# The last stage of a two-layer graph model: weights and two blocks of rows loaded during attention, projections one block further ahead

## The chip, the core and the metric

The kernel runs on one core of a Trainium2 chip. The metric is device time in microseconds (us); less is better. The engines are named as in the profile: PE is the matrix engine (PEld its weight loads, which overlap), DVE the vector engine, ACT the scalar engine, POOL the GpSimd engine, and SP the engine that issues nearly all DMAs here. Each engine runs its own instructions in order, and engines wait for one another by semaphores. SBUF is the on-chip memory, PSUM the small memory into which PE writes[...].

## The reference

A graph attention network of two layers is followed by one masked transformer layer. The change lies in the transformer layer, which is computed from x, the output of the graph layers (4096 rows of 256):

```
qkv = layer_norm(x, g1, be1) @ w_qkv              # 8 heads of 32
scores = einsum('nhd,mhd->hnm', q, k) * SCALE
scores = where(adj != 0, scores, -inf)
attn = softmax(scores, axis=-1)
out = einsum('hnm,mhd->nhd', attn, v).reshape(n, 256)
x = x + out @ w_proj + b_proj
h2 = layer_norm(x, g2, be2)
ff = gelu(h2 @ w1 + b1) @ w2 + b2                 # 256 -> 1024 -> 256
return x + ff
```

## The kernel before

The first half of the time goes to the graph layers, which the change does not touch. The transformer layer is the function `unshifted_transformer`. It works on the 4096 rows in eight blocks of 512 (`NNB`, `NB`), and on the eight heads in two halves of four (`DC`, `HC`). There are three parts.

**Queries, keys and values.** For each block, PE multiplies the normed rows by the weights (L1668, L1687). Queries and keys are split into a high and a low fp16 half and written to DRAM (`half_d`). From there `stack` reads the keys back into one large tile, `k_st`, of 128 partitions by 8 heads by 4096 columns: two DMAs of 32 partitions for each block (L1624), each followed by a copy on DVE to the 32 partitions beside it (L1701). Values stay in `v_sb`. In this part the order of SP's instructions is the written one.

**Attention.** The work is cut into 512 units: block of queries `nb`, half of the heads `c`, and one of 32 tiles of 128 keys `mt`. For each unit and each pair of heads (`u`), `weights` does eight matmuls into PSUM (L1725), an exponential on ACT (L1732) and a product with the mask on DVE (L1734), which gives a tile `u_e` (a ring of ten). POOL adds the tiles of two units that follow each other into `u_both` (L1816, a ring of six), except for two pairs of every sixteen. PE then multiplies `u_e` by the values (`u_av`) and `u_both` by ones (`u_dn`), both at L1743; a list, `waiting`, interleaves these with later units' scores. At the end of each half of the heads ACT copies both sums out; the numerators go to `att_d` in DRAM (L1760), the denominators to `den_d` (L1778). Two later steps read the denominators back in another shape (L1781) and invert them on DVE and store them in `inv_d` (L1785, L1786). The order on PE, ACT and DVE is the written one; on SP and POOL it is set by the scheduler of the language, which works with its own estimates of durations. All 512 units have the same length, so one half of the heads of one block takes about 73 us. Query tiles (`u_q`) and masks (`u_mask`) have rings of two and five buffers; the masks are read in four chunks per block.

**The last stage.** After attention, the projection weights, the biases and the feed-forward weights are loaded (L1840 to L1898; the projection weights twice). For each block `rows_of` issues six DMAs: the rows of x (L743, `u_xres`), the attention numerators (L1861, `u_att`) and four with the inverted denominators, spread over the partitions (L1866, `u_wide`). `projected` adds the projection bias on POOL (L1874), multiplies numerators and inverses on DVE (L1875), does 16 projection matmuls (L1879), adds the result to the rows (L1886) and norms them: the mean on DVE (L1447, L1448), squares on ACT (L1455), a square root on ACT (L1462), reciprocal and scaling on DVE (L1473, L1475). POOL then adds the second bias (L1889). `turned` transposes the normed rows on PE (L1488), evicted by ACT (L1491). In the profile a matmul of fp32 counts as two, so 16 written ones appear as 32.

The loop over blocks is written like this: the projection of block `nb + 1`, whose rows are also loaded there; 16 matmuls into the hidden layer (L1915) with a gelu on ACT (L1922); the transposes of block `nb + 1`; 32 matmuls out of the hidden layer (L1931) with an add on DVE (L1938) and stores on SP (L1939). Before the loop block 0 is projected and transposed. The order in this stage is the scheduler's on all engines, and what it chose on PE is, for each block: hidden layer, transposes of the next block, output layer, projection of the block after the next one.

```
        res, res_n = projected(*first)
        hn = turned(res_n)
        for nb in range(NNB):
            more = nb + 1 < NNB
            if more:
                res_next, res_n = projected(*rows_of(nb + 1))
```

Tiles of a pool with two buffers (`u_xres`, `u_att`, `u_wide`) can be loaded only when the block two before has let go of them; for `u_xres` this is when its output has been stored.

Of the kernel before, what the change touches and what calls it, by code (L numbers as in the profile page):

```python
# [8 lines left out]
F32 = mybir.dt.float32  # L9
BF = mybir.dt.bfloat16  # L10
F16 = mybir.dt.float16
# [1547 lines left out]
def unshifted_transformer(  # L1559
# [46 lines left out]
    nc.vector.memset(ones, 1.0)  # L1606
    dens = wts.tile([P, NQ, QI], F32, name="u_dens")


    with ExitStack() as scope:  # L1610
        vals = scope.enter_context(tc.tile_pool(name="u_vals", bufs=1))
        k_st = vals.tile([P, DC * HC, N], F16, name="u_k")
        v_sb = vals.tile([P, NT, D], F32, name="u_v")
        blocks = scope.enter_context(tc.tile_pool(name="u_blocks", bufs=2))
        masks = scope.enter_context(tc.tile_pool(name="u_masks", bufs=5))
        block_tiles = {}

        def stack(to, i, order, cols):

            for a, kind in enumerate(order):  # L1620
                if kind is None:
                    continue
                first = half_d[i, kind, 0, 0:1, cols]
                nc.sync.dma_start(  # L1624
                    to[a * O : (a + 1) * O],
                    spread(first, [[N, O], [O * N, DC * HC], [1, NB]]),
                )

        def load_queries(nb):
            q_st = blocks.tile([P, DC * HC, NB], F16, name="u_q")  # L1630
            stack(q_st, 0, (0, 1, 0, 1), slice(nb * NB, (nb + 1) * NB))
            block_tiles[nb] = q_st, []
# [9 lines left out]
        with ExitStack() as qkv:  # L1642
# [8 lines left out]
            for nb in range(NNB):  # L1651
# [44 lines left out]
                for b in (nb - 1,) if nb + 1 < NNB else (nb - 1, nb):  # L1696
                    if b >= 0:
                        at = slice(b * NB, (b + 1) * NB)
                        stack(k_st[:, :, at], 1, (0, None, 1, None), at)
                        for o in (0, 2 * O):  # L1700
                            nc.vector.tensor_copy(k_st[o + O : o + 2 * O, :, at], k_st[o : o + O, :, at])  # L1701
                    if b == 0:
                        load_queries(0)
# [12 lines left out]
        def weights(nb, c, mt, u):  # L1716

            q_st, chunks = block_tiles[nb]
            mask = chunks[mt // MC][:, mt % MC, :].unsqueeze(1).to_broadcast([P, 2, NB])
            ps = ps_s.tile([P, 2, NB], F32, name="u_ps")  # L1720
            for j in range(2):
                h = c * HC + 2 * u + j
                for r in range(HC):
                    at = mt * P + r * O
                    nc.tensor.matmul(  # L1725
                        ps[r * O : (r + 1) * O, j, :],
                        k_st[:, h, at : at + O],
                        q_st[:, h, :],
                        start=True,
                        stop=True,  # L1730
                    )
            nc.scalar.activation(ps, ps, AF.Exp, scale=SCALE)  # L1732
            e = work.tile([P, 2, NB], F32, name="u_e")
            nc.vector.scalar_tensor_tensor(e, mask, 0.0, ps, op0=ALU.not_equal, op1=ALU.mult)  # L1734
            return e
# [55 lines left out]


        units = [(nb, c, mt) for nb in range(NNB) for c in range(DC) for mt in range(NT)]
        es_of = {}
# [10 lines left out]
        for i in range(len(units) + 5):  # L1805
            for u in range(HC // 2):
                if i < len(units):
                    nb, c, mt = units[i]
                    if u == 0 and c == DC - 1 and mt % MC == 2 and nb + 1 < NNB:
                        if mt < MC:  # L1810
                            load_queries(nb + 1)
                        load_chunk(nb + 1, mt // MC)
                    es_of.setdefault(i, []).append(weights(*units[i], u))
                    if i % 2 == 1 and not alone(mt):
# [10 lines left out]
                for _ in range(min(count, len(waiting))):  # L1825
                    waiting.pop(0)()
            if i % 2 == 0 and later:
                later.pop(0)()
# [5 lines left out]
    with ExitStack() as scope:  # L1834
# [3 lines left out]
        ps_m = scope.enter_context(tc.tile_pool(name="u_ps_m", bufs=8, space=PSUM))  # L1838
        wp_sb = big.tile([P, DC, D], F32, name="u_wp")
        nc.sync.dma_start(wp_sb, w_proj.rearrange("(c p) e -> p c e", p=P))  # L1840

        def by_row(src, name):
            t = big.tile([P, D], F32, name=name)
            nc.sync.dma_start(t, spread(src, [[0, P], [1, D]]))
            return t.unsqueeze(1).to_broadcast([P, TB, D])

        bp_sb = by_row(b_proj, "u_bp")
        wp_sb = big.tile([P, DC, D], F32, name="u_wp")
        nc.sync.dma_start(wp_sb, w_proj.rearrange("(c p) e -> p c e", p=P))


        inside = big.tile(list(dens.shape), F32, name="u_inside")
        nc.vector.tensor_scalar(inside, dens, DEN_MIN, DEN_MAX, op0=ALU.max, op1=ALU.min)
        nc.vector.tensor_tensor(inside, inside, dens, op=ALU.is_equal)
        nc.vector.tensor_reduce(checks.column(), inside, AX.XY, ALU.min)

        def rows_of(nb):
            res = tail.tile([P, TB, D], F32, name="u_xres")
            rows.load(res, nb * TB)
            att = tail.tile([P, DC, NB], F32, name="u_att")  # L1860
            nc.sync.dma_start(  # L1861
                att, att_d[:, :, nb * NB : (nb + 1) * NB].rearrange("c p n -> p c n")
            )
            inv = tail.tile([P, DC, NB], F32, name="u_wide")
            for j in range(HC):
                nc.sync.dma_start(  # L1866
                    inv[j * O : (j + 1) * O],
                    spread(inv_d[nb * DC, j : j + 1, :], [[0, O], [HC * NB, DC], [1, NB]]),
                )
            return res, att, inv  # L1870

        def projected(res, att, inv):

            nc.gpsimd.tensor_tensor(res, res, bp_sb, op=ALU.add)  # L1874
            nc.vector.tensor_tensor(att, att, inv, op=ALU.mult)  # L1875
            for t in range(TB):
                pp = ps_m.tile([P, NB], F32, name="misc")
# [13 lines left out]


        first = rows_of(0)
        b2_sb = by_row(b2, "u_b2")
        w1_sb = big.tile([P, DC, F], F32, name="u_w1")
        nc.sync.dma_start(w1_sb, w1.rearrange("(c p) f -> p c f", p=P))
        w2_sb = big.tile([P, FC, D], F32, name="u_w2")
        nc.sync.dma_start(w2_sb, w2.rearrange("(c p) e -> p c e", p=P))  # L1898
        def turned(res_n):
# [4 lines left out]

        res, res_n = projected(*first)
        hn = turned(res_n)
        for nb in range(NNB):
            more = nb + 1 < NNB
            if more:
                res_next, res_n = projected(*rows_of(nb + 1))  # L1910
            hid = tail.tile([P, FC, NB], F32, name="u_hid")
# [13 lines left out]
            if more:  # L1925
                hn = turned(res_n)
            for t in range(TB):
# [13 lines left out]
                )  # L1941
            if more:
                res = res_next

# [109 lines left out]
```

## Time and profile before

| | us |
|---|---|
| median of 3 runs | 3249.26 (3246.59 to 3256.77) |
| profiled execution, its own time | 3250.22 |
| span of the profiled execution, first to last instruction | 3248.4 |
| PE busy | 3099.1 (95%) |
| DVE busy | 2804.6 (86%) |
| ACT busy | 2703.1 (83%) |
| POOL busy | 1177.5 (36%) |
| end of attention on PE, from the start of the span | 2946.4 |
| last matmul of the last stage ends | 3240.75 |

The times come from one execution that the hardware profiler recorded; they are counted from the start of its span. A row of the chain of work names a piece of work that ended just before the next one could start, so the pieces add up to the time. A row of the timeline gives the start, the length and the number of instructions that follow each other closely, and in brackets how long the engine stood idle before and who ended that. "SPq" is the issue of a DMA on SP, not its transfer. "Clock" is the share of PE's full clock that was granted.

### The profile page before, as it was taken

The page shows a single profiled execution, that of the slowest core. Times are in us where ns is not written, and L with a number is a line of the kernel's source. Part 1 is how long each engine was busy: PE and PEld are TensorE (multiplying, and loading weights), DVE is VectorE, ACT ScalarE, POOL GpSimd, SP SyncE. Part 2 cuts the span into 40 slices and gives each one's busy share as a digit, 9 for nine tenths or more (in the row PEclk, how much of TensorE's full clock was granted, in tenths as well). Part 3 has the DMA queues.
Part 4 walks back from the last instruction along what each step waited for, and adds up shares of the span by engine and source line. Part 5 has one row for each costly group of instructions (what it writes and reads, how often), then busy time and mean ns, then how long its engine had stood idle before and what let it go on. Part 6 is the DMA issues. An engine that isn't in the chain of part 4 may idle for free.

```text
span 3248.4 us, 139142 instructions
## 1 busy us (share of the span) xinstructions
PE 3099.1 (95%) x64076; PEld 2717.4 (84%) x64076; DVE 2804.6 (86%) x3102; ACT 2703.1 (83%) x3305; POOL 1177.5 (36%) x536
## 2 busy tenths in 40 slices
PE   5899999999889999999988999999999999997999
PEld 4799999999779999999965888888888888885666
DVE  6899999988889999999966999999999999994121
ACT  5799999999679999999964888888888888884332
POOL 2300000000310000000002998999888998893110
PEclk8999999999999999999999999999999999998999
DMA  7666554420310213120145010101101010004200
GB/s 250 203 198 201 167 185 149 148 74 29 105 42 31 84 54 93 42 75 27 38 121 143 14 40 20 33 27 27 32 24 47 14 40 15 20 7 120 69 33 27
DMA packets 210306, 249.30 MB, mean 77 GB/s; under 512 B 87792, under 2 KB 131056, under 8 KB 209712
## 3 DMA queue, kind: packets, MB, share of 16 engines
q1 hardware_dynamic: 209712, 240.31, 24.1%
q8 instruction: 503, 8.24, 1.1%
q14 instruction: 91, 0.75, 0.1%
HBM read 197.80 MB, written 42.47 MB: 74 GB/s over the span
## 4 chain that ended last, share of the span: by engine, by line
PE 44%; ACT 4%; DVE 3%; DMA 2%; issue 1%; POOL 0%; SPq 0%; POOLq 0%; DVEq 0%; ACTq 0%
PE u_ps L1725 15%; PE u_av L1743 14%; PE u_dn L1743 8%; PE misc L1931 3%; ACT t L1100 2%; PE misc L1668 2%; PE misc L1915 1%; PE misc L1687 1%; DMA u_xres<-rows 1%; DVE t L1102 1%; DVE t L1115 1%; PE misc L1488 1%; ACT ln_square L1455 0%; POOL u_xres L1874 0%; PE misc L1879 0%
## 5 line engine op out<-in xcount | busy, mean ns | idle before, releaser
L1401 PE MATMUL bank<-vst,t 128*128 128x132 f16 x16384 | 1451.0, 220 | 32.0 <-DVE t L1115 31.5
L1816 POOL TENSOR_TENSOR u_both<-u_e 128x1024 f32<-128x1024 f32 x448 | 1052.5, 2391 | 934.0 <-DVE u_e L1734 931.7
L1401 PE MATMUL bank<-vst,mask 128*128 128x66 f16 (+1 forms) x10296 | 1345.3, 206 | 0.0
L1100 ACT ACTIVATE t<-s_b,g_terms 128x1024 int8<-128x1024 f32 x1231 | 1318.9, 1154 | 27.6 <-PE bank L1401 21.7
L1401 PEld LDWEIGHTS <-t 128*128 128x128 fp8e4 x16384 | 1183.5, 97 | 47.1 <-DVE t L1115 36.6
L1734 DVE SCALAR_TENSOR_TENSOR u_e<-u_mask,u_ps 128x1024 f32<-128x1024 uint8 x1024 | 1165.9, 1215 | 10.3 <-ACT u_ps L1732 6.9
L1732 ACT ACTIVATE u_ps<-u_ps 128x1024 f32<-128x1024 f32 x1024 | 1030.1, 1009 | 142.1 <-PE u_ps L1725 44.0
L1401 PEld LDWEIGHTS <-mask 128*128 128x128 fp8e4 x10296 | 903.5, 98 | 0.0
L1115 DVE SCALAR_TENSOR_TENSOR t<-mask,t 128x2048 int32<-128x2048 int32 x256 | 591.3, 2310 | 82.6 <-ACT t L1100 72.4
L1725 PE MATMUL u_ps<-u_q,u_k 128*32 128x512 f16 x8192 | 637.1, 383 | 11.9 <-DVE u_e L1734 11.2
L1743 PE MATMUL u_av<-u_e,u_v 128*32 128x128 f32 x16384 | 601.8, 273 | 0.6 <-issue 0.6
L1743 PEld LDWEIGHTS u_av<-u_e,u_v 128*32 128x32 f32 x16384 | 488.9, 110 | 129.5 <-issue 2.6
L1102 DVE TENSOR_SCALAR t<-s_b,g_terms 128x1024 fp8e4<-128x1024 f32 x817 | 583.8, 747 | 2.6 <-DMA s_b<-s_d 2.6
L1035 POOL TENSOR_TENSOR vst<-g_prod,vst 128x528 f16<-128x528 f32 x36 | 44.2, 1244 | 777.8 <-DVE vst L1034 757.4
L1743 PE MATMUL u_dn<-u_both,u_ones 128*32 128x128 f32 x7168 | 280.2, 273 | 0.0
L1725 PEld LDWEIGHTS <-u_k 128*32 128x32 f16 x8192 | 228.6, 95 | 57.4 <-issue 16.2
L1743 PEld LDWEIGHTS u_dn<-u_both,u_ones 128*32 128x32 f32 x7168 | 212.9, 110 | 41.1 <-issue 0.5
L1922 ACT ACTIVATE u_hid<-misc,n_b 128x512 f32<-128x512 f32 x64 | 42.7, 682 | 149.5 <-PE misc L1915 149.5
L1938 DVE TENSOR_TENSOR u_xres<-u_xres,misc 128x256 f32<-128x256 f32 x32 | 13.5, 421 | 121.1 <-PE misc L1931 121.1
L1931 PE MATMUL misc<-u_w,u_hid 128*128 128x256 f32 x512 | 111.8, 379 | 0.0
L1915 PE MATMUL misc<-ln_cols,u_w 128*128 128x512 f32 x256 | 111.2, 592 | 0.0
L1931 PEld LDWEIGHTS misc<-u_w,u_hid 128*128 128x128 f32 x512 | 96.8, 190 | 13.2 <-issue 0.5
(147 smaller groups left out, 1916.4 us busy)
## 6 DMA issues: line engine op xcount, KB each, us to landing
g_adj<-in_adj_dram SPq DMA_DIRECT2D x123, 512.0 KB
s_b<-s_d SPq DMA_DIRECT2D x64, 512.0 KB
mask<-mask SPq DMA_DIRECT2D x128, 256.0 KB
u_mask<-mask SPq DMA_DIRECT2D x32, 512.0 KB
mask<-stage SPq DMA_DIRECT2D x48, 256.0 KB
rows<-e_x SPq DMA_DIRECT2D x32, 256.0 KB
half_d<-u_halves SPq DMA_DIRECT2D x32, 256.0 KB
u_q<-half_d SPq DMA_DIRECT2D x32, 256.0 KB
```

The source lines that it names most:

```text
L1100: nc.scalar.activation(to.bitcast(I8), s, AF.Sign, bias=negd, scale=-1.0)
L1102: nc.vector.tensor_scalar(to, s, negd, -1.0, op0=ALU.is_ge, op1=ALU.mult, saturate=False)
L1115: nc.vector.scalar_tensor_tensor(both, m32.unsqueeze(1).to_broadcast(list(both.shape)), SIGNS, both, op0=ALU.bitwise_or, op1=ALU.bitwise_and,)
L1401: nc.tensor.matmul(to, left, right, start=k not in opened, stop=last)
L1668: nc.tensor.matmul(pq, wq_sb[k][:, i * D + c * P : i * D + (c + 1) * P], hn[:, k, :], start=(k == 0), stop=(k == DC - 1),)
L1725: nc.tensor.matmul(ps[r * O : (r + 1) * O, j, :], k_st[:, h, at : at + O], q_st[:, h, :], start=True, stop=True,)
L1732: nc.scalar.activation(ps, ps, AF.Exp, scale=SCALE)
L1734: nc.vector.scalar_tensor_tensor(e, mask, 0.0, ps, op0=ALU.not_equal, op1=ALU.mult)
L1743: nc.tensor.matmul(to[j * O : (j + 1) * O, at], lefts[j], es[j // 2][:, j % 2, at], start=first and part == 0, stop=last and part == PARTS ...
L1816: nc.gpsimd.tensor_tensor(both, es_of[i - 1][u], es_of[i][u], op=ALU.add)
L1915: nc.tensor.matmul(ph, w1_sb[:, k, f * P : (f + 1) * P], hn[:, k, :], start=(k == 0), stop=(k == DC - 1),)
L1931: nc.tensor.matmul(po[:, :D], hid[:, f, at : at + P], w2_sb[:, f, :], start=(f == 0), stop=(f == FC - 1),)
```

## The change

The pools `u_blocks` (query tiles) and `u_masks` are kept open until the end, and the keys become two tiles, one for each half of the heads. The first lies in a pool of its own, `u_slab`. So each block's keys are stacked with four DMAs and four DVE copies of half the size, instead of two and two.

The second tile of `u_slab` takes the place of the first half's keys once these are no longer read, which is when the first half of the heads of the last block has its scores. `load_early` cuts it up and loads into it the projection weights, two biases, block 0's rows, numerators and inverses, and the feed-forward weights. Block 1's are loaded into a query buffer and a mask buffer that the last block doesn't use. POOL adds the projection bias to the rows of both blocks and multiplies numerators and inverses during attention; the duplicate load of the projection weights goes. ACT takes one square root of a single column ahead of its last two copies of attention.

In the last stage PE's order is now the written one. Blocks 0 and 1 are projected at once, block 0 is transposed, and then the loop projects block `nb + 2` ahead of the hidden layer of block `nb`, and loads block `nb + 3`. `u_xres` has four buffers. The checks of the denominators (`inside`) are written behind the first transposes.

In the scheduled program the instructions that the scheduler places stand so. On SP block 1's six loads stand behind the last block's mask loads, and before the stores of block 6's last sums. The loads of the slab up to block 0's inverses stand behind the next inverses' store; w1 stands behind the numerators' store of the last block's first half, and w2 between the four denominator stores (L1794) and the denominator load (L1797) of that half. On POOL the product for block 1 stands behind the first two sums (L1868) of the last block's first half; the two bias adds (L1882) stand ahead of the first two sums of its second half, and the product for block 0 (L1885) behind these two.

```diff
+    rooted = wts.tile([P, 1], F32, name="u_rooted")
+    slab_p = ctx.enter_context(tc.tile_pool(name="u_slab", bufs=1))
+    blocks = ctx.enter_context(tc.tile_pool(name="u_blocks", bufs=2))
+    masks = ctx.enter_context(tc.tile_pool(name="u_masks", bufs=5))
+    def load_rows(nb, res, att, inv):
+        rows.load(res, nb * TB)
+        nc.sync.dma_start(att, att_d[:, :, nb * NB : (nb + 1) * NB].rearrange("c p n -> p c n"))
+        for j in range(HC):
+            nc.sync.dma_start(
+                inv[j * O : (j + 1) * O],
+                spread(inv_d[nb * DC, j : j + 1, :], [[0, O], [HC * NB, DC], [1, NB]]),
+            )
...
-        k_st = vals.tile([P, DC * HC, N], F16, name="u_k")
+        k_st = [
+            pool.tile([P, HC, N], F16, name=f"u_k{c}") for c, pool in enumerate((slab_p, vals))
+        ]
...
-                        stack(k_st[:, :, at], 1, (0, None, 1, None), at)
-                        for o in (0, 2 * O):
-                            nc.vector.tensor_copy(k_st[o + O : o + 2 * O, :, at], k_st[o : o + O, :, at])
+                        for c in range(DC):
+                            stack(k_st[c][:, :, at], 1, (0, None, 1, None), at, c, HC)
+                            for o in (0, 2 * O):
+                                nc.vector.tensor_copy(
+                                    k_st[c][o + O : o + 2 * O, :, at], k_st[c][o : o + O, :, at]
+                                )
...
+        def load_early():
+            slab = slab_p.tile([P, 32 * D], F32, name="u_k0")
...
+            early["wp"] = piece(DC, "p (c e) -> p c e", c=DC)
+            nc.sync.dma_start(early["wp"], w_proj.rearrange("(c p) e -> p c e", p=P))
+            for name, src in (("bp", b_proj), ("b2", b2)):
+                early[name] = piece(1, "p (o e) -> p o e", o=1)
+                nc.sync.dma_start(early[name][:, 0], spread(src, [[0, P], [1, D]]))
+            two = blocks.tile([P, 2, TB * D], F32, name="u_q")
+            early[0] = (
+                piece(TB, "p (t d) -> p t d", t=TB),
+                piece(TB, "p (c n) -> p c n", c=DC),
+                piece(TB, "p (c n) -> p c n", c=DC),
+            )
+            early[1] = (
+                two[:, 0].rearrange("p (t d) -> p t d", t=TB),
+                two[:, 1].rearrange("p (c n) -> p c n", c=DC),
+                masks.tile([P, DC, NB], F32, name="u_mask"),
+            )
+            for nb in range(2):
+                load_rows(nb, *early[nb])
+            early["w1"] = piece(FC, "p (c f) -> p c f", c=DC)
+            nc.sync.dma_start(early["w1"], w1.rearrange("(c p) f -> p c f", p=P))
+            early["w2"] = piece(FC, "p (f e) -> p f e", f=FC)
+            nc.sync.dma_start(early["w2"], w2.rearrange("(c p) e -> p c e", p=P))
...
+                    if u == 0 and units[i] == (NNB - 1, DC - 1, 4):
+                        load_early()
...
+            for k, unit in enumerate(((NNB - 1, DC - 1, NT // 2 - 1), units[-1])):
+                if i < len(units) and units[i] == unit:
+                    res, att, inv = early[k]
+                    nc.gpsimd.tensor_tensor(
+                        res, res, early["bp"].to_broadcast([P, TB, D]), op=ALU.add
+                    )
+                    nc.gpsimd.tensor_tensor(att, att, inv, op=ALU.mult)
+            if i == len(units) - 1:
+                nc.scalar.activation(rooted, norms.eps, AF.Sqrt)
...
         def rows_of(nb):
-            res = tail.tile([P, TB, D], F32, name="u_xres")
+            res = tail.tile([P, TB, D], F32, name="u_xres", bufs=4)
...
+            load_rows(nb, res, att, inv)
             nc.gpsimd.tensor_tensor(res, res, bp_sb, op=ALU.add)
             nc.vector.tensor_tensor(att, att, inv, op=ALU.mult)
+            return res, att
...
-        res, res_n = projected(*first)
-        hn = turned(res_n)
+        scope.enter_context(tc.manual_schedule(engines={mybir.EngineType.PE}))
+        ready = [projected(*early[nb][:2]) for nb in range(2)]
+        coming = rows_of(2)
+        hn = turned(ready[0][1])
...
         for nb in range(NNB):
+            res, res_n = ready.pop(0)
             more = nb + 1 < NNB
-            if more:
-                res_next, res_n = projected(*rows_of(nb + 1))
+            if nb + 2 < NNB:
+                ready.append(projected(*coming))
+                if nb + 3 < NNB:
+                    coming = rows_of(nb + 3)
...
             if more:
-                hn = turned(res_n)
+                hn = turned(ready[0][1])
```

In the changed kernel the projection matmuls are at L1917, the hidden layer at L1957, the output layer at L1973, its adds at L1980, and the reciprocal of the denominators at L1801.

## The prediction

> **What bounds the kernel now.** I read the page's chain first, then the chain in order of time around the end of attention, then windows and timeline there. On the page the chain that ended last is matmul work almost throughout:
>
> ```profile
> PE 44%; ACT 4%; DVE 3%; DMA 2%; issue 1%; POOL 0%; SPq 0%; POOLq 0%; DVEq 0%; ACTq 0%
> ```
>
> So TensorE decides, and a change pays where TensorE stands still. Two windows (length, then busy us and count of PE, PEld, DVE, ACT, POOL, then clock, DMA share, GB/s) compare attention with what follows it:
>
> ```profile
> 2880.00:2909.00 29.00, 29.00 (x828) 22.78 (x822) 29.00 (x28) 25.81 (x26) 25.74 (x12) 1.00 0.02 5
> 2949.00:2966.00 17.00, 5.46 (x13) 4.37 (x14) 3.74 (x8) 0.00 (x0) 2.34 (x1) 0.51 0.75 245
> 3000.00:3240.00 240.00, 233.01 (x862) 159.15 (x861) 43.39 (x101) 74.97 (x134) 28.19 (x12) 1.00 0.14 44
> ```
>
> Attention has PE and DVE both full and POOL nearly so; the start of the last stage is empty and at half clock; the rest of it is 97% PE. The chain in order of time (start, us, what) across the seam and one later block:
>
> ```profile
> 2944.64 1.78 PE u_dn L1743 x62
> ...
> 2947.96 5.24 DMA den_d<-u_den
> 2953.28 1.75 DMA u_dens<-den_d
> 2956.66 3.88 DMA u_b<-in_L_gnn_b_dram
> 2960.54 6.60 PE misc L1879 x16
> ...
> 2976.16 5.63 PE misc L1879 x16
> 2981.79 13.73 PE misc L1915 x32
> 2995.52 0.88 PE misc L1488 x8
> 2996.39 13.83 PE misc L1931 x64
> ...
> 3012.55 3.96 DMA u_xres<-rows
> 3016.67 2.36 POOL u_xres L1874
> 3028.86 1.63 PE misc L1488 x8
> 3030.49 13.83 PE misc L1931 x64
> ```
>
> Attention ends at 2946.4; the first feed-forward matmul (L1915) starts at 2981.8, 35.4 us later, behind denominators, weights, two projections and a layer norm. Thereafter each block's transposes (L1488) wait for a norm whose rows were loaded only after the previous block's output: 2996.4 to 3030.5 is 34.1 us of pitch.
>
> **The last stage, step by step.** Let 0 be attention's end. With weights and both blocks' inputs in place, the first projection needs only the copy of the denominators out of PSUM (0.59, done at 0.65). At full clock 16 projection matmuls take 3.62 (PE timeline at 3010.05), so projections 0 and 1 end at 4.3 and 7.9. DVE adds (0.42 each) end for block 0 at 4.8; mean 1.23, one add of block 1 in between, scaling 0.18: 6.7. Four squares at 0.63: 9.2. The square root's table load (1.28) has been moved ahead of the last copies, where ACT sat idle 3.7 us in the old trace, so the root takes 0.3: 9.6. Meanwhile DVE finishes block 1's adds and mean at 9.65. Reciprocal, scaling, two norm pieces (0.35 each), the last reciprocal of denominators (its data arrived 8.6 after attention's end in the old trace; it isn't late), two more pieces: 11.7. Transposes end near 12.2.
>
> PE's order then puts the projection of **block 2** ahead of block 0's feed-forward. Its attention product stands on DVE behind four small checks (1.5 in all, to 13.2) and block 1's norm; the latter waits for ACT, which does block 1's squares and block 0's two evictions (0.72 each) first: root at 14.55, norm to 16.2, product 1.22 to 17.45. Its loads were issued from 2.3 on; the last quarter follows the reciprocal and should land near 13, hidden.
>
> PE has by then been almost idle for 5 us or more. After the old seam the granted clock read 0.5 from 2949.3, and with work from 2960.5 it recovered at 2966.4, 5.9 us later. By that row block 2's projection runs at half clock, 5.6 to 6.6 as in the two rows above; I take 6.1, and feed-forward starts at **23.6**. [...] Thus 35.4 - 23.6 = **11.8** saved.
>
> The third projection is then already done, where the old kernel had done two: one of 3.28 (3010.22 to 3013.50) fewer remains: **3.3**.
>
> From L1915's start to PE's last L1931 (3240.75) the old stage took 258.96. Its pieces are 8 x 13.73 + 8 x 13.83 + 7 x 0.88 + 6 x 3.28 = 246.3, so 12.6 were waits for rows and norms. Afterwards projection runs two blocks ahead, the norm of block nb+1 has some 30 us, and ACT's 12.6 us per block (8 x 0.68, 4 x 0.69, two table loads, root, two evictions) fits the 32 us pitch. The new order has one snag, a gelu table load waiting for the first hidden tile, 1.28 late[...]. I take all **12.6**; if only the first half of the waits goes it is 6. The tail of 7.65 us stays. Sum: 11.8 + 3.3 + 12.6 = **27.7**.
>
> **What is put into attention.** The early loads are 17 DMAs on SP (6 for block 1's rows, attention and inverses; 3 small weights; 6 for block 0; two of 1 MB) and four POOL operations. Block 1's six wait for the last scores of block 6 (2793.3) and its mask buffer (2796.0); 1.5 MB at some 200 to 350 GB/s land by about 2801. POOL's product stands after the first pair of sums of the last block, which ended at 2804.2: no wait. The other eleven wait for the last scores of the first half of the heads, at 2866.6. POOL must then do two adds before the first pair of the last half, and the product after it. The cover is POOL's lead over TensorE:
>
> ```profile
> 2872.81 12.00 POOL L1816 TENSOR_TENSOR u_both<-u_e 128x1024 f32<-128x1024 f32 x5 [3.73 <-DVE u_e L1734]
> 2877.63 28.20 POOL L1816 TENSOR_TENSOR u_both<-u_e 128x1024 f32<-128x1024 f32 x12
> 2904.87 0.41 PE L1743 MATMUL u_dn<-u_both,u_ones 128*32 128x128 f32 x8
> ```
>
> POOL works back to back until 2905.83 (seven pairs); the sixth ends 4.7 earlier, at 2901.1, and PE uses it at 2904.87: 3.7 us of slack, the smallest of the series (4.6 at the first). A lone 512 KB load took 3.96, of which 1.5 is its bytes at 350 GB/s and 2.4 the rest; so I estimate the biases landed at 2870.2 (384 KB ahead) and block 0's rows at 2872.1 (1 MB); two adds of 2.36 end at 2875.0, the pair starts 2.2 late, and the product makes it 4.5. That exceeds the slack by **0.8**. PE, DVE and ACT are all full here, so this is not won back within the run of seven pairs; the idle 3.7 us in front of the next run stops it from growing. Loads landing 2 us late would make it 2.8; prompt ones, nothing.
>
> The second queue moved past is the denominators' round trip. Behind DVE's reciprocal stand all further mask products:
>
> ```profile
> 2880.04 0.34 SPq L1781 DMA_DIRECT2D u_dens<-den_d  x1
> 2885.66 0.25 DVE L1785 RECIPROCAL u_inv<-u_dens 128x16 f32<-128x16 f32 x1
> ```
>
> In the new order one megabyte stands before the four small stores and one before the load. At the 350 to 386 GB/s that the windows of 2961 to 2967 show for such loads each takes 3 us: stores land about 2880.3, the load about 2884, before 2885.7: nothing. At the 200 GB/s of the slower windows it lands at 2887.8, a 2.1 us stall.
>
> **The split of the keys.** 16 more issues at 0.47 on SP and 16 more copies on DVE. During the QKV products SP and DVE idle between blocks (SP spent 7.1 us on four issues, waiting), so nothing. But six full copies, 1.22 each, stood amid the first attention units, where DVE was busy 9.85 of 10 us. Halves cost between 0.61 and 1.22; with DVE's smallest operation, 0.17, as the fixed part it is 0.70: 12 x 0.70 - 6 x 1.22 = **1.1** lost. Finer pieces reach the first products sooner and two copies were stretched to 3.2 and 2.0 by other traffic, so the bounds are a gain of 2 and a loss of 4. The duplicate projection-weight load vanishes, off the path.
>
> **Sum.** 27.7 - 0.8 - 1.1 = 25.8. Against the profiled execution's span of 3248.4 this gives 3222.6, against its time of 3250.2, 3224.4. That time lies 1.0 above the median of the runs shown, 3249.3, so the forecast for a median is **3223.5**.
>
> **Rivals.** (1) *Attention pays more*: POOL's extra operations or the denominators come 3 to 8 us late, for 3227 to 3232. For: three engines are full, little slack. Against: DMA stood at 2 to 14% in those rounds. (2) *The waits per block stay*, moved to other loads or to the norm's chain: gain 11.8 + 3.3 - 1.9 = 13.2, for 3236. For: every load still shares one SP queue. Against: four row buffers and a whole block of lead. (3) *It doesn't do what it says*: the loads land no earlier, because their buffers come free late; then only small shifts are left, about 3247. Against: the changed program's SP order has them directly behind the previous denominators. (4) *Slower*: the denominator load stuck behind the early megabytes stalls DVE before most of the last half's products. It costs 1 us per us and decides from 25.8 us of stall on, that is, landing after 2911.5: 4 MB in 45 us, 90 GB/s. The trace had four times that; with a landing at 2920 it is 3258.
>
> **How the numbers follow.** The forecast 0.72, rival 1 0.13, rival 2 0.09, rival 3 0.03, rival 4 0.03. Change of under 0.3% (about 10 us) can't be told from none here: faster 0.94, same 0.03, slower 0.03. Clock and unhidden copies move the likeliest case between 3217 and 3228; the range of 3217 to 3230 takes in part of rival 1.
>
> **What would show it.** Right: L1917 starts within 1 us of attention's end; the first L1957 about 24 us after it; transposes from then on without waits, block pitch 31.7; the rounds before the end as long as 73.4, at most 75. Wrong: idle DVE at its second-last reciprocal of denominators, u_dn waiting for POOL, or L1957 later than 30 us after attention's end.

## The result, and the profile after

The changed kernel takes 3229.66 us (median of 6 runs, 3226.87 to 3232.19) against 3248.62 us of the kernel before (6 runs, 3246.59 to 3256.77): a ratio of 0.9938, 95% interval 0.9926 to 0.9951. That is 19.0 us faster, where 25.8 were forecast; the time lies inside the range, near its upper end of 3230 and 6.2 us above the predicted 3223.5. The profiled execution has a span of 3227.2 us.

On the page of the changed kernel the chain that ended last has more matmul and less waiting in it:

```profile
PE 47%; DVE 3%; ACT 2%; issue 1%; DMA 0%; SPq 0%; DVEq 0%; ACTq 0%
```

Three windows answer the three of before (the columns are the same: length, busy us and count of PE, PEld, DVE, ACT, POOL, clock, DMA share, GB/s). The first is the same stretch of attention, the second the 17 us around the seam, the third the rest of the last stage:

```profile
2880.00:2909.00 29.00, 27.61 (x787) 23.87 (x779) 27.62 (x26) 25.09 (x26) 29.00 (x13) 1.00 0.25 81
2953.50:2970.50 17.00, 9.29 (x39) 7.15 (x38) 12.83 (x27) 6.52 (x20) 7.81 (x3) 0.80 0.68 188
2975.00:3213.00 238.00, 238.00 (x879) 162.32 (x878) 46.03 (x98) 82.83 (x145) 22.14 (x10) 1.00 0.14 41
```

The last stage now has no idle PE at all, and the seam is half full. But attention, which had PE busy for all of its 29 us, now has a hole of 1.4 us, and 787 matmuls instead of 828. The chain in order of time across the seam and one block (start, us, what):

```profile
2949.32 1.79 PE u_dn L1759 x64
...
2951.18 0.59 ACT u_den L1792
...
2951.82 7.19 PE misc L1917 x32
...
2962.52 2.54 DVE u_inside L1944
...
2967.26 1.14 DVE u_att L1909
...
2968.45 6.35 PE misc L1917 x16
2974.80 13.73 PE misc L1957 x32
2988.53 0.87 PE misc L1488 x8
2989.41 13.82 PE misc L1973 x64
3003.22 3.45 PE misc L1917 x16
3006.68 13.73 PE misc L1957 x32
3020.41 0.87 PE misc L1488 x8
3021.28 4.75 PE misc L1973 x22
```

Attention ends at 2951.11 and the first hidden matmul starts at 2974.80, 23.7 us later (35.4 before). From 2989.41 to 3021.28 is a pitch of 31.9, without a wait.

So the stages behind attention gave what was forecast, and attention took part of it back. Where, is seen by taking the end of the last score matmul of each of the sixteen rounds (a round is one half of the heads of one block) from the two traces: before, the last two rounds take 73.35 us each; after, **77.42 and 76.69**, 7.4 us more. The other terms, before minus after, in one account of the span: 2.9 us before attention begins (graph layers and QKV; not counted as the change's, since over all twelve kernels here this point lies between 1752.1 and 1755.2, changed or not), -1.0 in the first round, +0.7 in rounds 2 to 14, -7.4 in the last two, +11.7 in the seam, +15.2 in the last stage, -0.9 in its tail; sum 21.2. Without the 2.9 it is 18.3, near the 19.0 of the medians.

The waits of PE from 2700 to 2953, attention's last part, name a releaser that the kernel before doesn't have there (from 2700 to 2945 it has no row in this view):

```profile
PE u_av L1759 <- issue: 2.9, 2, 1.5
PE u_dn L1759 <- issue: 2.5, 1, 2.5
PE misc L1917 <- ACT u_den L1792: 0.7, 1, 0.7
```

"Issue" means that PE waited for nothing that the profile knows of: no semaphore, no data. The windows around the longest of these show that the DMA engines were busy just before, and the clock afterwards:

```profile
2795.00:2799.00 4.00, 4.00 (x129) 3.47 (x125) 4.00 (x5) 3.28 (x5) 2.17 (x1) 1.00 0.84 181
2799.00:2803.00 4.00, 1.53 (x49) 1.33 (x44) 2.37 (x3) 1.24 (x2) 3.51 (x3) 1.00 0.24 79
2803.00:2807.00 4.00, 4.00 (x77) 3.72 (x72) 2.00 (x2) 2.52 (x3) 4.00 (x3) 0.57 0.03 8
2807.00:2811.00 4.00, 4.00 (x127) 3.88 (x123) 3.38 (x4) 3.74 (x4) 2.48 (x2) 1.00 0.04 6
```

DMA share 0.84 comes from block 1's six early loads (1.5 MB, issued at 2790.67 to 2795.1). Then PE stands for 2.47 us, and its clock falls to 0.57 for 4 us: 77 matmuls in place of 127, another 1.6 us. Together 4.07, which is the whole loss of that round. The page lists two DMA queues of a kind "instruction", to which no line of the kernel issues (packets, MB, share of 16 engines' span):

```profile
q8 instruction: 503, 8.24, 1.0%
q14 instruction: 92, 0.75, 0.1%
```

Queue 8 carries nearly all of it, in 503 packets of 16,384 bytes. During attention the trace has one every 4.54 us (median), and in the changed kernel none begins between 2791.07 and 2799.22, a gap of 8.15. I took this for a sign of the cause, and had three theories:

**Theory 1.** The early loads cost the time because they are issued as a burst: packets of queue 8 come late beside them, and PE stands beside late packets. **Theory 2** is the prediction's own rival: the four POOL operations make the sums `u_both` late. **Theory 3**: any transfer slows the matmuls in proportion to its bytes.

### The profile page after: what moved, and what is told of

It reads as the page before. It is cut to its first block, busy times and chain, and to the rows that moved or that the text cites. A ratio compares the mean times of both kernels' runs of the same rounds, so it can differ in the third digit from the quotient of the medians.

```text
span 3227.2 us, 139159 instructions
## 1 busy us (share of the span) xinstructions
PE 3091.4 (96%) x64076; PEld 2718.0 (84%) x64076; DVE 2810.0 (87%) x3116; ACT 2701.1 (84%) x3304; POOL 1181.2 (37%) x538
## 4 chain that ended last, share of the span: by engine, by line
PE 47%; DVE 3%; ACT 2%; issue 1%; DMA 0%; SPq 0%; DVEq 0%; ACTq 0%
PE u_ps L1741 15%; PE u_av L1759 14%; PE u_dn L1759 8%; PE misc L1973 3%; PE misc L1957 3%; ACT t L1100 2%; PE misc L1681 2%; PE misc L1917 1%; PE misc L1700 1%; DVE t L1102 1%; DVE t L1115 1%; PE misc L1488 0%; DMA u_mask<-mask 0%; PE bank L1401 0%; ACT adj L1455 0%
## 5 line engine op out<-in xcount | busy, mean ns | idle before, releaser
L1868 POOL TENSOR_TENSOR u_both<-u_e 128x1024 f32<-128x1024 f32 x448 | 1051.6, 2391 | 928.8 <-DVE u_e L1750 926.8
L1401 PEld LDWEIGHTS <-t 128*128 128x128 fp8e4 x16384 | 1182.9, 96 | 46.6 <-DVE t L1115 36.6
L1741 PE MATMUL u_ps<-u_q,u_k 128*32 128x512 f16 x8192 | 640.2, 383 | 11.7 <-DVE u_e L1750 11.0
L1980 DVE TENSOR_TENSOR u_xres<-u_xres,misc 128x256 f32<-128x256 f32 x24 | 10.1, 421 | 124.9 <-PE misc L1973 124.9
L1973 PE MATMUL misc<-u_k,u_hid 128*128 128x256 f32 x512 | 111.8, 380 | 0.0
L1957 PE MATMUL misc<-ln_cols,u_k 128*128 128x512 f32 x256 | 111.2, 593 | 0.0
L1973 PEld LDWEIGHTS misc<-u_k,u_hid 128*128 128x128 f32 x512 | 96.9, 190 | 13.1 <-issue 0.5
```

Source lines behind the costliest of these rows:

```text
L1401: nc.tensor.matmul(to, left, right, start=k not in opened, stop=last)
L1741: nc.tensor.matmul(ps[r * O : (r + 1) * O, j, :], k_st[c][:, 2 * u + j, at : at + O], q_st[:, h, :], start=True, stop=True,)
L1868: nc.gpsimd.tensor_tensor(both, es_of[i - 1][u], es_of[i][u], op=ALU.add)
L1957: nc.tensor.matmul(ph, w1_sb[:, k, f * P : (f + 1) * P], hn[:, k, :], start=(k == 0), stop=(k == DC - 1),)
L1973: nc.tensor.matmul(po[:, :D], hid[:, f, at : at + P], w2_sb[:, f, :], start=(f == 0), stop=(f == FC - 1),)
```

## The experiments

All numbers on rounds below are worked out from the traces like those above; "seam" is attention's end to the start of the first hidden matmul record, "stage" from there to the end of the last output matmul (before 35.2 and 259.1, changed kernel 23.6 and 243.9). The first four kernels have one time each, 3253.97, 3251.85, 3255.66 and 3225.96 us, beside 3246.15 for the kernel before; since six runs of the kernel before alone lie between 3246.59 and 3256.77, these times settle nothing of a few us, and the rounds are read instead.

**Loads alone, of several sizes.**

```diff
+        bursts = {
+            (1, 0, 10): lambda: att_load(1, 0, 0),
+            (2, 0, 10): lambda: [row_load(2, 0, 4, TB), att_load(2, 1024, 1)],
+            (3, 0, 10): lambda: w1_load(3),
+            (5, 0, 10): lambda: [w1_load(5), w1_load(5, False)],
+            (7, 0, 10): lambda: [row_load(7, 0, 4, TB), att_load(7, 1024, 1), wide_load(1)],
+        }
+        for k in range(8):
+            bursts[4, 0, 10 + k] = lambda k=k: row_load(4, k * D, 4 + k, 1)
+        for k in range(4):
+            bursts[6, 0, 10 + k] = lambda k=k: att_load(6, k * NB, 1, NB)
```

> The kernel before, plus loads whose data nobody reads, put into the query buffer that is idle in the first round of each block (a one-column copy on ScalarE holds each in its place): block 1: 512 KB in one load; block 2: 512 KB of rows and 512 KB of attention at once; block 3: w1, 1 MB in one load; block 4: eight loads of 128 KB, one per unit; block 5: w1 twice, one behind the other, 2 MB; block 6: four loads of 256 KB, one per unit; block 7: the six loads of block 1, 1.5 MB at once, as the changed kernel has them. No operation on POOL, DVE or PE is added. Theory 1 [...]: the round of block 7 grows by 3 to 5 us (the changed kernel's had +4.1), that of block 5 by as much or more, blocks 2 and 3 by 0 to 3, blocks 1, 4 and 6 by under 0.5; each longer round shows idle time of PE put down to issue and a gap in the packets of the instruction queue of over 6 us instead of 4.5. Theory 2 (the operations on POOL make the sums late): no round grows by over 0.3. Theory 3 (any transfer slows the matmuls themselves): rounds grow in proportion to their bytes, paced ones too, about 2.7 us for each MB.

Measured, first round of each block against the same round of the kernel before (the scheduler put the next block's queries, 1 MB, 3 to 5 us behind each of the first six, where they had stood apart before; so the loads that came together there are larger than the column says):

| block | extra load | round grew by | PE idle, put down to issue | longest gap of queue 8 |
|---|---|---|---|---|
| 1 | 512 KB | 1.0 | 0.91 | 6.70 |
| 2 | 512 + 512 KB | 0.6 | 0.56 | 6.74 |
| 3 | 1 MB | 0.8 | 0.84 | 6.04 |
| 4 | 8 x 128 KB, one per unit | -0.8 | none | 5.07 |
| 5 | 1 MB, then 1 MB | 2.4 | 2.21 + 0.27 | 6.63 |
| 6 | 4 x 256 KB, one per unit | 0.7 | 0.27 | 6.25 |
| 7 | 1.5 MB, block 1's six loads | 0.9 | 0.65 | 7.32 |

The kernel before has losses of its own in blocks 2 to 6 (0.2 to 0.8). Against 73.34, the shortest round of any kernel here, the seven rounds are longer by 1.1, 0.8, 1.0, 0.0, 2.8, 0.9 and 0.9. Waits of PE from 1800 to 2950 in this kernel (total, times, longest):

```profile
PE u_av L1790 <- issue: 5.7, 7, 2.2
```

Theory 2 falls as the only cause: nothing was added on POOL, and rounds grow. Theory 3 falls: 1 MB in pieces of 128 KB cost nothing (73.34 in block 4). Theory 1 has the kind right and sizes wrong: the same six loads as in the changed kernel cost 0.9 us here, not 3 to 5, and blocks 1 and 6, expected under 0.5, lost 1.0 and 0.7. The stand isn't as long as the packet is late, and the difference varies: in the changed kernel the gap was 8.15 - 4.54 = 3.6 us over the median and PE stood for 2.47, 1.1 less; here it was 2.8 over and PE stood for 0.65, 2.1 less. And no clock drop followed: 1.00 was granted from 2822 to 2834.

**POOL alone.**

```diff
+            n = {(NNB - 1, 0, 2): 1, (NNB - 1, 0, NT - 1): 2, (NNB - 1, 1, 2): 1}
+            if i < len(units) and units[i] in n:
...
+                for _ in range(n[units[i]]):
+                    nc.gpsimd.tensor_tensor(junk, v_sb[:, :TB, :], v_sb[:, TB : 2 * TB, :], op=ALU.mult)
```

> The kernel before, plus the four operations on POOL alone (128x1024 float32, result never read, one in the first round of the last block, two at its end, one early in the second), without any load. Theory 1 [...]: both last rounds stay at 73.3 to 73.5, no idle time of PE put down to issue. Theory 2 (POOL makes the sums late): the changed kernel's +4.1 and +3.3 us, 7.4 in all, come back in these two rounds. The prediction's own sum had 0.8 here.

Measured: both rounds within 0.01 of 73.34, nothing lost; PE has no wait from 2700 to 2930. The operations stood where the changed kernel has them (L1834, POOL's timeline):

```profile
2867.66 4.86 POOL L1834 TENSOR_TENSOR u_q<-u_v 128x1024 f32<-128x1024 f32 x2
2872.47 4.73 POOL L1817 TENSOR_TENSOR u_both<-u_e 128x1024 f32<-128x1024 f32 x2
2877.14 2.39 POOL L1834 TENSOR_TENSOR u_q<-u_v 128x1024 f32<-128x1024 f32 x1
```

Two adds ran in the idle time before the first pair. In the changed kernel each of them had to wait for a load first, and stood later:

```profile
2872.65 2.37 POOL L1882 TENSOR_TENSOR u_q<-u_q,u_k 128x1024 f32<-128x1024 f32 x1 [2.11 <-DMA u_k<-in_L_gnn_b_proj_dram]
2876.98 2.38 POOL L1882 TENSOR_TENSOR u_k<-u_k 128x1024 f32<-128x1024 f32 x1 [1.96 <-DMA u_k<-rows]
```

So this experiment shows that the four operations cost nothing here when their data are there, not what their waits cost; that is read below.

**The split keys alone.**

```diff
-        k_st = vals.tile([P, DC * HC, N], F16, name="u_k")
+        k_st = [vals.tile([P, HC, N], F16, name=f"u_k{c}") for c in range(DC)]
```

> The kernel before with the keys in two tiles and nothing else of the change (32 more DMA issues and 16 more copies on DVE before and at the start of attention). Theory 1: the first round grows by 1.0 us, the other fifteen by nothing (within 0.1 each), time +1.0. Rival: the later rounds also read keys from two tiles and drift, by the 0.7 us that the changed kernel lost from before to after round 13, or the last two rounds are longer by the 7.4.

(The trace counts 16 more issues, 32 in place of 16, not 32 more.) Measured: the first round 84.18 against 83.08, +1.1; the other fifteen lost 0.3 in sum, the last two nothing (73.34 each). The single time is worse by more than that: the seam took 37.6 and the stage 262.3 here. The two kernels above, with the last stage untouched as well, had 35.6 and 36.6, 261.2 and 260.7: the old last stage varies by some 3 us from run to run with its waits for loads. The changed stage took 243.9 in every kernel that kept its order.

**Early loads written behind attention.**

```diff
-                    if u == 0 and units[i] == (NNB - 1, DC - 1, 4):
-                        load_early()
...
+        load_early()
+        for k in range(2):
+            res, att, inv = early[k]
+            nc.gpsimd.tensor_tensor(res, res, early["bp"].to_broadcast([P, TB, D]), op=ALU.add)
+            nc.gpsimd.tensor_tensor(att, att, inv, op=ALU.mult)
```

> The changed kernel with all its early loads and its four operations on POOL put behind attention (buffers, order and the projection two blocks ahead are kept). Theory 1: the last two rounds fall back to 73.35 each, attention is 7.4 us shorter; from its end to the first matmul of the hidden layer some 36 to 40 us instead of 23.7 (the kernel before had 35.4; here two blocks are projected first); the rest of the stage stays at 243.8. Time 3227 + 14 - 7.4 = 3234 or so. If the last two rounds stay at 77, loads and POOL have nothing to do with it and the split tiles or the code's size have.

The edit didn't do what it was for: the order on SP and POOL is the scheduler's, and it issued the loads as soon as their buffers came free (2790.8 and 2864.7), as in the changed kernel. So it is a second sample of the same loads: rounds of 73.90 and 77.86, seam 22.6, time 3225.96 (one run). Nearly the same loads at the start of block 7 cost 0.6 us here and 4.1 in the changed kernel; the gap of queue 8 was 6.04 instead of 8.15.

**Pieces of at most 256 KB, one per unit; and of 128 KB.** Each is held at its unit by a copy of one column on ACT:

```diff
+        def touched(to, src):
+            at = to[:, :1] if len(to.shape) == 2 else to[:, 0, :1]
+            nc.scalar.copy(at, ones[: to.shape[0], :1])
+            nc.sync.dma_start(to, src)
...
+                    if u == 1 and units[i] in paced:
+                        paced.pop(units[i])()
```

> The changed kernel with its early loads cut into pieces of at most 256 KB, one issued per unit (each held there by a one-column copy on ScalarE); the operations on POOL stand where the sums leave a gap, behind loads that have landed by then; everything else as changed. Theory 1 [...]: little or no idle time of PE put down to issue, gaps of the instruction queue under 6.3 us; of the 7.4 us that the last two rounds lost at least 5 come back (four loads of 256 KB in this rhythm cost a round of the first experiment some 0.5 us). Seam and feed-forward stage unchanged (23.7, 243.8): 3222 to 3225 us. Rival (it is the bytes, not their bunching): the two rounds stay at 77 each and the time at 3229.

> As the paced kernel, with pieces of 128 KB (12 in the first of the last two rounds, 30 in the second, the last two of w2 behind attention). Theory 1: like the eight loads of 128 KB in the first experiment: gaps of the instruction queue under 5.6 us, no idle time of PE put down to issue, both rounds at 73.3 to 73.6: 7 us faster than the changed kernel, 3222 us or less. Rival (bytes): as the changed kernel, 3229.

Measured: 3226.24 us (ratio 0.9930, 0.9917 to 0.9944) for 256 KB, rounds 73.35 and 76.12; 3224.00 (0.9923, 0.9910 to 0.9937) for 128 KB, rounds 73.34 and **73.94**. Both medians lie above what was expected (3222 to 3225, and 3222 or less). In neither is a PE wait put down to issue in these rounds: for the pieces of 128 KB the view from 2700 to 2945 has no row. Of the 7.4 us, 6.8 are back in the rounds of the trace, with all but the last 256 KB of w2 still loaded during attention. By the medians it is 5.7, and 4.4 beside the second measurement of the changed kernel below; all five times (3221.72 to 3224.64) lie under all eleven of the changed kernel (3226.85 to 3232.19). The edit moved the four POOL operations too, but POOL can't be the rival here: the lost time was put down to issue, and the loads alone lost time without any of these operations. It was the bunching. What remained with 256 KB is mostly another cause, in the second half of its last round (waits from 2866 to 2945):

```profile
DVE u_e L1750 <- POOL u_both L1921: 2.5, 3, 1.2
```

Here POOL itself was late: the product of block 0, put in the middle of the round by my edit, started at 2904.56 with the next sums behind it. This is the prediction's rival at work, for some 2.2 of the 2.8 us (0.6, in units 14 to 18 of the round, are lost with 128 KB as well), in a kernel whose PE never waits for issue there.

**The order in the seam.**

```diff
-            if nb + 2 < NNB:
-                ready.append(projected(*coming))
-                if nb + 3 < NNB:
-                    coming = rows_of(nb + 3)
             hid = tail.tile([P, FC, NB], F32, name="u_hid")
...
+            if nb + 2 < NNB:
+                ready.append(projected(*coming))
+                if nb + 3 < NNB:
+                    coming = rows_of(nb + 3)
             if more:
                 hn = turned(ready[0][1])
```

> The changed kernel with the projection of block nb+2 moved in the written order from before the hidden layer of block nb to behind it (ahead of the transposes of block nb+1); loads as changed. The prediction's step: the projection of block 2 at half clock stands in the seam for 6.1 us. If that is so: end of attention to first hidden matmul 16 to 18 us instead of 23.7; the projection returns behind the hidden layer at 3.5 to 3.6 us at full clock; the pitch stays 31.9; in all 3 to 4 us less than the changed kernel, 3225 to 3227 us. If instead the normed rows of block 0 bound the seam, it shortens by under 3 us and the time stays within 1 us of 3229.

Measured: 3224.82 us (0.9922, 0.9909 to 0.9936). The seam is 12.6 us instead of 23.6, the stage 249.8 instead of 243.9: 5.0 gained in the trace, 4.8 by the medians (3 to 4 expected, with a seam of 16 to 18). PE's timeline:

```profile
2962.52 2.38 PE L1488 MATMUL misc<-ident,ln_rows 128*128 128x128 f32 x8 [2.33 <-DVE ln_rows L1475]
2964.91 16.31 PE L1953 MATMUL misc<-ln_cols,u_k 128*128 128x512 f32 x32
2981.06 3.62 PE L1917 MATMUL misc<-u_k,u_att 128*128 128x256 f32 x16
```

against, in the changed kernel:

```profile
2968.45 6.35 PE L1917 MATMUL misc<-u_k,u_att 128*128 128x256 f32 x16 [5.34 <-DVE u_att L1909]
2974.64 13.90 PE L1957 MATMUL misc<-ln_cols,u_k 128*128 128x512 f32 x32
```

More than the projection at half clock stood in the seam: PE also waited 5.34 us for that block's attention product, with block 0's normed rows ready. Moved behind, the projection takes 3.62. The slow clock stays: 0.50 was granted from 2964 to 2968 and 0.60 from 2968 to 2970, and the first hidden layer now takes 16.31 instead of 13.90 us.

**Both together.** The 128 KB pieces and this order:

> The pieces of 128 KB and the projection behind the hidden layer together. If both causes are independent, the gains add: some 10 to 11 us less than the changed kernel, 3218 to 3220 us.

Measured: **3218.03 us** (0.9906, 0.9891 to 0.9921), rounds 73.34 and 73.97, seam 12.7. By the medians it is 11.6 below the changed kernel; the two gains by themselves, 5.7 and 4.8, make 10.5, so they add.

**The changed kernel again, and the query loads in pieces.** The second adds to the kernel just told:

```diff
-            stack(q_st, 0, (0, 1, 0, 1), slice(nb * NB, (nb + 1) * NB), 0, DC * HC)
...
+            for k in range(2 * HC):
+                paced[nb - 1, DC - 1, (3, 4, 5, 6, 7, 8, 9, 11)[k]] = (
+                    lambda a=k % HC, c=k // HC: quarter(a, c)
+                )
```

> The changed kernel once more, nothing edited, beside the next one on the same chip. Theory 1: the last two rounds are again longer than 73.4 by several us in sum (between 4 and 8), with idle time of PE put down to issue that ends 1.3 to 1.6 us after a late packet of the instruction queue has landed; the split between the two rounds may differ[...]. Time 3226 to 3232.

> The kernel with pieces of 128 KB and the projection behind the hidden layer, and in addition the query loads of every block (1 MB at once, in the kernel before as well) cut into eight loads of 128 KB, one per unit. Theory 1: rounds 3 to 14 of the kernel before carry small losses of the same kind (73.5 to 74.1 instead of 73.34, some 2 us in sum); they go, no gap of the instruction queue over 5.6 us between the first round and the last: 1.5 us less, 3216.5. Rival: those losses have another cause (masks, memory) and stay; 3218.

Measured: the changed kernel 3228.36 us (0.9935, 0.9922 to 0.9949); its last two rounds 73.69 and 77.34. So the loss is there again, but 4.3 us this time, nearly all in the last round (block 1's loads cost 0.3). With the queries in pieces **3216.58 us** (0.9899, 0.9884 to 0.9914), the fastest of all. Rounds 3 to 14 sum to 880.4 us there, 881.4 without this edit and 882.0 in the kernel before; the shortest possible, 12 of 73.34, are 880.1. The kernel before thus had some of the same loss; its waits of PE from 1800 to 2945 have one row, which is gone with the pieces:

```profile
PE u_av L1743 <- issue: 0.6, 1, 0.6
```

The intervals of the last two kernels overlap, so the 1.45 us between their medians aren't shown by the times, only by the rounds; and the expectation on the gaps failed: some up to 6.15 us remained, without a stand of PE.

## Why the prediction was right and wrong

The decisive evidence for theory 1 is a coincidence that repeats. Over these kernels there are 13 stands of PE in attention, behind its first round, of more than 0.6 us that end neither with POOL nor with another engine's data. In 12 of them PE resumes 1.28 to 1.61 us after a packet of queue 8 has landed, in one 0.92, and that packet or the one before it came late. In the changed kernel:

| PE resumes | idle | packet landed | before that |
|---|---|---|---|
| 2801.85 | 2.47 | 2800.43 | 1.42 |
| 2876.14 | 1.51 | 2874.65 | 1.49 |
| 2882.07 | 1.39 | 2880.78 | 1.29 |

None of these packets was slow by more than 0.4 us itself: they took 1.21, 0.99 and 1.37 us, where the median is 0.99. They began late, 8.15, 7.44 and 5.76 us after the packet before them. The loads alone lost time without POOL (0.6 to 2.4 us a round, in all rounds but that with pieces of 128 KB), POOL alone lost none, and with the pieces of 128 KB 6.8 of the 7.4 us were gone with nearly all bytes kept. So it was bunched loads that cost the time, with late packets beside the stands. How a late packet and a stand of PE hang together was not shown.

The records don't name the engine that the packets go to; the counts are these. The page of the changed kernel has 64,076 matmuls, 64,076 weight loads and 503 packets, 255 of PE's instructions to one packet. From 400 to 800 us, in the graph layers, there are 15,160 to 60 packets, from 2300 to 2700, in attention, 22,999 to 90: 253 and 256, although PE has half as many again in the second stretch. DVE and ACT have fewer there than in the first (354 and 359 against 424 and 429; with their semaphore instructions DVE has 522 against 517 and ACT 727 against 508), and POOL has none in the first. So in these two stretches the number of packets goes with PE's instructions; which engine they serve was not shown.

Point by point, by the prediction's steps:

- **Seam, 11.8:** 11.7. The stations were met: the first two projections end 7.9 after attention (7.9), the transposes at 12.0 (12.2), block 2's product at 17.3 (17.45), its projection takes 6.35 at half clock (6.1), first hidden matmul 23.7 (23.6). Taking the clock from the old trace's row (back 5.9 us after the work began) came out right: the projection ran from 2968.45, and the granted clock came back 5.4 us later, at 2973.8.

```profile
2971.00:2973.00 2.00, 2.00 (x6) 1.55 (x6) 0.47 (x2) 0.00 (x0) 2.00 (x2) 0.50 0.30 97
2973.00:2975.00 2.00, 2.00 (x8) 1.55 (x7) 0.58 (x2) 0.00 (x0) 2.00 (x1) 0.80 0.00 0
```

One station was met partly by luck: ACT's root was done 13.7 after attention, not 14.55, but DVE used it only at 14.6, because one check (L1944) took 2.53 us where it had taken 0.42 in the kernel before. A better order was missed, worth 5.0.
- **Third projection and per-block waits, 15.9:** 15.2. All waits went; rival 2 is refuted. The late gelu table load (2976.60, 1.28 us) cost PE nothing: the first hidden layer's 32 matmuls ran 13.90 us from 2974.64 without a wait. The tail, "stays 7.65", became 8.6.
- **Split keys, 1.1:** 1.0, and 1.1 with the split alone. The first round is not quite fixed: one kernel with split keys took 83.0 and one without 81.0.
- **The denominators' round trip, 0:** right. DVE's reciprocal ran without an idle moment, though 4.5 us later than before, with everything else:

```profile
2884.45 5.77 DVE L1750 SCALAR_TENSOR_TENSOR u_e<-u_mask,u_ps 128x1024 f32<-128x1024 uint8 x5 [1.12 <-ACT u_ps L1748]
2890.14 0.24 DVE L1801 RECIPROCAL u_inv<-u_dens 128x16 f32<-128x16 f32 x1
```

- **POOL's four operations, 0.8:** about 0.3. Comparing the start of each unit's scores in the last 64 units with those of before, the loss comes in three places: 4.1 within units 2 to 6 after block 1's loads, 3.0 in units 34 to 38 after those into the keys' buffer, and 0.3 in units 46 to 50. The last is put down to POOL; this is argued, not tested. In the repeated run the part behind POOL is some 1 us or less, and its border to the rest is not sharp.
- **What failed is the step "what is put into attention".** It asked of the early loads only who waits for their data, and where SP's queue delays another DMA; 5.5 MB were costed at nothing beyond that. Against rival 1 it held that DMA stood at 2 to 14%, but that was the share without its own loads, which raised it to 0.84 for 4 us. The missing term is 7.1 us in the profiled run (5.4 idle, 1.6 of half clock after the longest stand, 0.1 unassigned) and about 3 to 4 in the repeated one.

The forecast of 25.8 minus this term is 18.7; 19.0 was measured. The time fell where rival 1 had put it, 3227 to 3232, "attention pays more", but neither of the two mechanisms that it named, POOL or the denominators, did it in the main. So the gain behind attention was foreseen term by term, while the loss in attention was covered only by the width of the range, which took in part of rival 1 for another reason: that is luck. The prediction's own sign shows it. The rounds before the end were to take 73.4 us, at most 75; they took 77.42 and 76.69.

What stays open: why the same six loads cost between 0.3 and 4.1 us. The gap of queue 8 differs (6.04 to 8.15 us), and so does what the stand falls short of the lateness (1.1 to 2.1). No run here controlled where in the queue's 4.54 us rhythm a burst began.

## What to carry to other kernels

"The DMA queues are nearly empty there" (2 to 14% in the prediction) didn't make the loads free: the same 1.5 MB, issued at once, cost a round between 0.3 and 4.1 us. Where loads are put beside an engine that is always busy (PE here, with 828 matmuls in 29 us of attention before), try pieces of about 128 KB, one every 2.3 us (a unit here), which cost no stand of PE in the last two rounds. The sign in this trace was a wait of PE put down to "issue" (2.47 us), next to a DMA share of 0.84 and a gap of 8.15 us in a queue of the kind "instruction". When work of a later block is pulled ahead, look for what it now stands in front of: here the first hidden layer stood behind a projection that waited 5.34 us for its product, and putting the layer first gave 4.8 us by the medians.

## What the runs showed of the hardware

- Packets of 16,384 bytes on queue 8, of the kind "instruction", came once for every 253 to 256 of PE's instructions, every 4.54 us in this attention; with 1 to 1.5 MB of loads issued at once the gap grew to between 6.0 and 8.2 us. In the two cases compared, PE stood 2.47 us beside a packet that was 3.6 late and 0.65 beside one that was 2.8 late; in 12 of 13 stands it went on 1.3 to 1.6 us after a packet had landed.
- After the stand of 2.47 us the granted clock was 0.57 over 4 us, from 2803 to 2807. Around the stands of 1.51 and 1.39 us in the same kernel (2874 to 2886) and of 0.91, 2.21 and 0.65 in the one with the loads alone it stayed at 1.00.
- A one-column copy on ACT, used to hold a load in its place, took 0.18 us. With 30 of them in one round, and POOL's operations, that round took 73.94 us instead of 73.35; which of the two the 0.6 belongs to wasn't separated.
